# A hybrid transformer layer whose instruction order a planner decides: the planner's constants and ranks, the way six batches are transposed, and the engine that writes a mask

## The chip, the cores and the metric

The kernel runs on one core of one Trainium2 chip, in one launch, all in float32. The metric is the device time of a run in microseconds (us). A separate execution was taken with the hardware profiler; its span runs from the first to the last instruction.

## The reference, cut to what matters

Eight sequences (batches) `x` of 256 tokens by 256 features pass through four residual steps, each on a layer norm of `x`:

```
x = x + attn_a(layernorm(x))   # 16 heads of 128: q, k, v, softmax, output projection
x = x + ffn(layernorm(x))      # gene lookup, see below
x = x + attn_b(layernorm(x))   # 16 heads of 16, rotary, causal mask by blocks of 64 tokens
x = x + ffn(layernorm(x))      # the same weights again
```

For each token, `ffn` computes 512 gene logits from the RMS-normed token, keeps the 32 largest, takes their softmax, sums the chosen gene vectors (32 numbers) with these weights, and multiplies `tanh(. Wd)`, the normed token and `. Wu`. With 256 tokens the block mask of `attn_b` comes down to this: a query of an earlier block of 64 doesn't see a later block.

## The kernel before, in words

**Tiling.** A batch is two tiles (t = 0, 1) of 128 tokens by 256 features. The tiles of a batch are `x[b, t]`. Each step of a batch depends on the step before it, so TensorE is kept busy by running attention A of later batches beside the gene layers (`ffn`, layer 0 and layer 2) and block attention (`attn_b`, layer 1) of earlier ones.

**Who sets the order.** Every operation is first recorded by `do(...)` (L297) with its engine, a cost in ns (how long it occupies the engine, and when its result can be used), the keys it reads and writes, its buffers and a rank. `Plan.order` (L129) then walks through a model of the five queues (PE, DVE, ACT, POOL, SP) and picks, engine by engine, the operation of lowest rank among those that could start within `WAIT` of the earliest. The instructions are emitted in that order and every engine executes its own list strictly in order. So the constants of the model time nothing on the chip, but they decide which instruction stands before which. In the model a consumer on another engine may start `HOP` after its producer's end (and `LOAD` later on PE); a consumer on the same engine (L203) as soon as the engine is free. A DMA lands its transfer time (bytes over `SCATTER` for the trips below) plus `FLIGHT` after it starts to move. `keep_warm` (L213) puts idle transposes of the identity (L1392) where the model leaves PE idle for over 800 ns and a PSUM bank is free.

**Ranks.** PE ranks of attention A are its batch plus the share of heads done (0 to 8). Those of the gene layers and of block attention stand in `PE_RANK`, nearly all negative, so they go first on PE as soon as the model calls them ready. `EW_RANK` does the same for the operations on the other engines and on SP: a small number goes ahead of attention A, one of 20 and more behind it.

**A DRAM trip** (`turn`, L494) transposes without TensorE. VectorE transposes each 128x512 tile in blocks of 32x32 (L510), SP sends four stripes to DRAM (D<-T, L519), and one DMA brings them back permuted (PT<-D, L528). Its flat form (L516, L526) serves a 256-wide normed tile: four stripes of 64 KB out, in pieces of 32 numbers, and four DMAs back. SP waits in order: an instruction that waits for a landing holds all behind it. Trips are used for attention A's probabilities (L708, read by the attend matmuls L721), for its normed input (AxT), for block attention's probabilities (L1265, read by L1292) and, for batches 0 to 4, for the gene weights (L954, read by L992).

**The gene layer** (`ffn` L937, `experts` L1045) has a chain per tile: statistics and norm (L461 to L480, two small steps on POOL); two PE transposes of the normed tile `Fxn` (L1054); a ScalarE copy out of PSUM (L1060); logits (L1068); four rounds of max-8 (L1078) and match-replace (L1095) on VectorE; one pass that keeps the chosen weights (L1100); their transposition; L992, L1012; then the gating (L1025 to L1041).

**Block attention** (`attn_b` L1120): transposes of `Rxn` (L1134), q and k (L1152), rotary on VectorE and POOL, scores of 4 groups (L1228). For each group VectorE then writes the mask's value into 64 rows of the score bank (L1242), takes the row maxima (L1344), and ScalarE the exponentials (L1350). The two tiles of a batch and all batches go through it one after the other (`lane`).

**The last batch** (b = 7) runs attention A tile by tile (L767): all of tile 0, then tile 1, whose last output projection is L876 and whose last addition to `x` is L884. Only the layers of batch 7, and whatever the order has left, come after it.

Of the kernel before, what the change touches and what calls it, by code (L numbers as in the profile page):

```python
# [17 lines left out]
P = 128  # L18
# [15 lines left out]
    [[-0.85, -0.85], [-0.84, -0.84], [-0.83, -0.83]],  # L34
    [[-0.82, -0.82], [7.03, -0.81], [8.72, -0.8]],
    [[7.78, -0.79], [8.7, -0.78], [7.32, -0.77]],
]
EW_RANK = [
    [[1.62, 1.49], [20.64, 2.07], [2.72, 20.2]],
    [[2.79, 3.31], [3.38, 3.19], [21.34, 1.84]],  # L40
    [[22, 4.66], [21.53, 22.1], [3.28, 4.32]],
    [[22.77, 23], [4.69, 23.1], [5.73, 23.2]],
    [[24.18, 5.62], [4.78, 23.98], [6.79, 4.31]],
    [[25.44, 6.57], [5.62, 7.27], [25.2, 7.37]],
    [[8.15, 6.17], [7.09, 26.01], [29.52, 26.55]],
    [[9.27, 8.68], [26.56, 26.64], [7.38, 9.82]],
# [26 lines left out]
class Plan:  # L73
# [4 lines left out]
    HOP = 65.0  # L78
    LOAD = 300.0
    DRAIN = 165.0  # L80
    FLIGHT = 2000.0
    RATE = 330.0
    SCATTER = 200.0
    OPEN = 8
    WAIT = {"PE": 50.0, "DVE": 50.0, "ACT": 100.0, "POOL": 200.0, "SP": 400.0}
# [43 lines left out]
    def order(self):  # L129
        engines = ("PE", "DVE", "ACT", "POOL", "SP")  # L130
        free = dict.fromkeys(engines, 0.0)
        ready = {e: [] for e in engines}
        slots = {}
        for o in self.ops:
            for b in o.bufs:
                slots.setdefault(b.tag, [(0.0, i) for i in range(b.bufs)])
                for i in range(b.bufs):
                    if b.pool is not None and (b.tag, i) not in self.tiles:
                        self.tiles[b.tag, i] = b.pool.tile(b.shape, F32, name=f"{b.tag}_{i}")
            if not o.left:  # L140
                ready[o.eng].append(o)
        done = []

        open_ = [0.0] * self.OPEN

        def start(o):
            t = max(free[o.eng], o.ready)
            if o.eng == "SP":
                t = max(t, open_[0])
            need = {}  # L150
            for b in o.bufs:
                if not b.held:
                    need[b.tag] = need.get(b.tag, 0) + 1
            for tag, n in need.items():
                have = slots[tag]
                if len(have) < n:
                    return None
                t = max(t, sorted(have)[n - 1][0])
            return t

        while len(done) < len(self.ops):
            best = None
            for e in engines:
                cand = [(t, o.pri, o) for o in ready[e] if (t := start(o)) is not None]
                if not cand:
                    continue
                now = min(c[0] for c in cand)
                pick = min((c for c in cand if c[0] <= now + self.WAIT[e]), key=lambda c: (c[1], c[2].n))
                if best is None or pick[0] < best[0]:
                    best = pick  # L170
            if best is None:
                raise RuntimeError("no operation can start: " + str([
                    (o.eng, o.pri, [(b.tag, b.held) for b in o.bufs])
                    for e in engines for o in ready[e]][:12])
                    + str({t: len(v) for t, v in slots.items()}))
            t, _, o = best
            ready[o.eng].remove(o)
            o.at = t
            for b in o.bufs:
                if not b.held:  # L180
                    b.held = True
                    have = slots[b.tag]
                    have.sort()
                    b.i = have.pop(0)[1]
                    b.slot = self.tiles.get((b.tag, b.i))
                    b.begin = t
            free[o.eng] = t + o.occ
            if o.eng == "SP":
                self.moved = max(self.moved, t) + o.lat
                end = self.moved + self.FLIGHT  # L190
                open_.append(end + self.HOP)
                open_.pop(0)
            else:
                end = t + o.lat
            for b in o.bufs:
                b.touch -= 1
                b.end = max(b.end, end)
                if not b.touch:
                    slots[b.tag].append((b.end + self.HOP, b.i))
                    self.taken.setdefault((b.tag, b.i), []).append((b.begin, b.end + self.HOP))  # L200
            for u in o.users:
                u = self.ops[u]
                same = u.eng == o.eng and o.eng != "SP"  # L203
                hop = self.HOP + (self.LOAD if u.eng == "PE" else 0.0)
                u.ready = max(u.ready, t + o.occ if same else end + hop)
                u.left -= 1
                if not u.left:
                    ready[u.eng].append(u)
            done.append(o)
        self.span = max(free.values())  # L210
        return done
# [27 lines left out]
def kernel(  # L239
# [44 lines left out]
    def dve(cols, half=False):  # L284
        occ = 70.0 + cols * (0.52 if half else 1.04)
        return occ, occ + 90.0

    def act(cols, ptr=False):
        occ = 60.0 + cols * 0.833 + (90.0 if ptr else 0.0)
        return occ, occ + 110.0  # L290
# [162 lines left out]
    def normed(b, t, who, ew, rms=False, xn=None, after=(), held=()):  # L453
# [7 lines left out]
            "DVE", (330, 420), lambda: [nc.vector.bn_stats(st(), x())],  # L461
            ew, [(x, 0), *((y, 0) for y in after)], [(st, 0)],
        )
        do("DVE", (90, 175), lambda: [nc.vector.bn_aggr(mv(), st())], ew, [(st, 0)], [(mv, 0)])
# [4 lines left out]
            "POOL", (220, 270),  # L469
# [4 lines left out]
            "POOL", (520, 560),  # L474
# [19 lines left out]
    def turn(sources, dst, n, pri, keys, flat=False):  # L494
# [8 lines left out]
        for j, (p, view) in enumerate(sources):  # L503
            def out(j=j):
# [4 lines left out]
                "DVE", dve(n * P),  # L509
# [23 lines left out]
    def normed_a(b):  # L533
# [35 lines left out]
        if b:  # L569
            for i, (a_, b_, f_) in enumerate((  # L570
# [4 lines left out]
                    "POOL", (480.0, 530.0),  # L575
# [320 lines left out]
    def softmax(sc, keys, p, n, k, who, ew):  # L896
# [9 lines left out]
        for i in range(n):  # L906
            do(
                "ACT", (155 + k * 0.83 + 92, 155 + k * 0.83 + 200),
                lambda i=i: [nc.scalar.activation(  # L909
                    p()[:, i, :], s3()[:, i, :], AF.Exp, bias=nm()[:, i : i + 1],  # L910
                    accum_out=sm()[:, i : i + 1])],
                ew, [*keys, (nm, 0)], [(p, ("e", i)), (sm, i)],
            )
        do(
            "DVE", (75, 165), lambda: [nc.vector.reciprocal(sm(), sm())],  # L915
# [21 lines left out]
    def ffn(b, ts_, layer):  # L937
# [8 lines left out]
        for t, xn, e, sm in zip(ts_, xns, es, sms):  # L946
            experts(
                b, t, layer, lambda stage, t=t: pe(stage, t), xn, e, sm, xns, es, [xs[b, i] for i in ts_])
# [47 lines left out]
        cost = 730.0 if n == 2 else 505.0  # L996
# [12 lines left out]
        cost = 1140.0 if n == 2 else 858.0  # L1009
# [11 lines left out]
    def gated(b, t, ew, pg, down, up, xn, sm):  # L1021
# [7 lines left out]
            "DVE", (390, 490),  # L1029
# [5 lines left out]
            b, t, 256, (700, 740),  # L1035
# [4 lines left out]
            b, t, 256, (690, 730),  # L1040
# [4 lines left out]
    def experts(b, t, layer, pe, xn, e, sm, xns, es, both):  # L1045
# [3 lines left out]
        normed(b, t, "F", ew, True, xn, both, xns)  # L1049
        xT = sb([P, DC, P], "FxT", 2)  # L1050
        pt = bank("B")
        do(
            "PE", (218.0, 218.0 + plan.DRAIN),
            lambda: (nc.tensor.transpose(pt()[:, ts(c, P)], xn()[:, ts(c, P)], ident)  # L1054
                     for c in range(DC)),
            pe(0), [(xn, 0)], [(pt, 0)], [xT, *es],
        )
        do(
            "ACT", act(256),
            lambda: [nc.scalar.copy(xT().rearrange("p c q -> p (c q)"), pt()[:, :S])],  # L1060
            ew, [(pt, 0)], [(xT, 0)],
        )
        pl = bank("B")
        left = sb([P, G], "Fleft", 2)
        for c in range(DC):
# [3 lines left out]
                    pl(), xT()[:, c, :], wcT[:, c, :], start=c == 0, stop=c == DC - 1)],  # L1069
                pe(1), [(xT, 0), ("wcT",)], [(pl, 0)], [left, *es],  # L1070
# [3 lines left out]
        for r in range(4):  # L1074
            src, key = (pl, (pl, 0)) if r == 0 else (left, (left, 0))
            do(
                "DVE", (600 if r else 640, 740 if r else 760),
# [3 lines left out]
            if r == 0:  # L1081
                do(
                    "DVE", (55, 150),
# [5 lines left out]
                    "ACT", (690, 800),  # L1089
# [4 lines left out]
                "DVE", (672, 755),  # L1094
# [4 lines left out]
            "DVE", (720, 820),  # L1099
# [4 lines left out]
        do("DVE", (75, 165), lambda: [nc.vector.reciprocal(sm(), sm())], ew, [], [(sm, 0)])  # L1104
# [6 lines left out]
    kbs = {}  # L1111
    VP = DIM + DB
# [7 lines left out]
    def attn_b(b, t):  # L1120
# [26 lines left out]
        for i, n in enumerate("qk"):  # L1147
# [12 lines left out]
            "DVE", (620, 720),  # L1160
# [11 lines left out]
            b, t, 512, (1235, 1280),  # L1172
# [6 lines left out]
            b, t, 512, (1230, 1275),  # L1179
# [4 lines left out]
        for par in range(2):  # L1184
            vec(
                b, t, 256, (460, 520),
# [26 lines left out]
        def scores(c, pT):  # L1213
# [7 lines left out]
            def emit():  # L1221
# [11 lines left out]
                "PE", (1200.0, 1200.0 + plan.DRAIN), emit, pe(3),  # L1233
# [4 lines left out]
            for g in range(NR):  # L1238
                sc, p = scs[g], ps_[g]
                do(  # L1240
                    "DVE", (n * 53 + 93, n * 53 + 180),
                    lambda sc=sc: [nc.vector.memset(  # L1242
                        sc()[0:BLOCK].rearrange("p (h k) -> p h k", h=n)[:, :, 512 // n - BLOCK :],
                        MASKED)],
# [35 lines left out]
        def attend(cs_, pT):  # L1280
# [17 lines left out]
            cost = 1200.0 if n * len(cs_) == 2 else 650.0  # L1298
# [39 lines left out]
    def softmax_b(sc, p, p3, n, k, ew):  # L1338
# [8 lines left out]
        for i in range(n):  # L1347
            do(
                "ACT", (155 + k * 0.83 + 92, 155 + k * 0.83 + 200),
# [6 lines left out]
            "DVE", (75, 165), lambda: [nc.vector.reciprocal(sm(), sm())],  # L1356
# [92 lines left out]
```

## Time and profile before

| | us |
|---|---|
| three runs, median (lowest, highest) | 959.45 (958.21, 959.88) |
| the profiled execution's own time | 960.78 |
| its span, first to last instruction | 959.0 |
| its time outside the span | 1.78 |
| TensorE clock granted, mean | 0.995 |

| engine | busy us | share of span |
|---|---|---|
| PE (matmul) | 919.5 | 96% |
| VectorE | 703.6 | 73% |
| ScalarE | 468.0 | 49% |
| POOL | 404.4 | 42% |
| DMA queue of SP | | 49.2% of 16 engines |

A matmul in float32 goes through PE in two passes, and each pass is one record; records of neighbours overlap, so PE's busy share is no measure of useful work. The distance from one start to the next is: 216 ns for a pass of 256 columns, 429 for one of 512, 110 for one of 128 or a transpose. Groups of instructions are shown as line, engine, operation, tiles, shape, count | busy us, mean ns of one | idle time of the engine just before them and what ended it.

### The profile page before, as it was taken

How to read it: one execution, taken by the hardware profiler on the slowest of the kernel's cores; microseconds unless marked ns; L12 is line 12 of the kernel's file. 1: busy time of each engine (PE TensorE's matmuls, PEld its weight loads, DVE VectorE, ACT ScalarE, POOL GpSimd, SP SyncE). 2: the span in 40 equal slices, each digit the busy share in tenths (PEclk: the TensorE clock that was granted, in tenths of full speed). 3: DMA queues.
4: the chain of work that ended last, by engine and by line, in shares of the span. 5: the costliest groups of instructions: out<-in, count | busy, mean ns of one | idle time of the engine just before them, and what ended most of it. 6: DMA issues, size and time to landing. Idle time of an engine off the chain costs nothing.

```text
span 959.0 us, 17226 instructions
## 1 busy us (share of the span) xinstructions
PE 919.5 (96%) x5815; PEld 737.7 (77%) x5815; DVE 703.6 (73%) x1716; ACT 468.0 (49%) x1550; POOL 404.4 (42%) x530
## 2 busy tenths in 40 slices
PE   7999999999999999999999999999999999999776
PEld 6878888887678777887678788877777877787564
DVE  2543484769967789669886884988788788868765
ACT  3534343754266544564455554465436643764461
POOL 4722224642176422662247343464237414743430
PEclk9999999999999999999999999999999999999989
DMA  9873333476337763485455746177525731550000
GB/s 324 248 209 94 110 106 115 123 221 173 111 111 200 202 166 105 131 231 174 135 143 171 200 133 190 44 208 216 148 67 163 211 106 40 147 173 1 6 7 12
DMA packets 109192, 136.09 MB, mean 142 GB/s; under 512 B 26288, under 2 KB 90416, under 8 KB 109104
## 3 DMA queue, kind: packets, MB, share of 16 engines
q1 hardware_dynamic: 109104, 134.99, 49.2%
q8 instruction: 46, 0.75, 0.3%
q14 instruction: 42, 0.34, 0.1%
HBM read 72.82 MB, written 62.13 MB: 141 GB/s over the span
## 4 chain that ended last, share of the span: by engine, by line
PE 56%; DVE 32%; issue 4%; DMA 3%; POOL 2%; ACT 2%; SPq 1%; DVEq 0%; ACTq 0%
PE ps L674 12%; DVE Fleft L1095 8%; DVE Fm L1078 7%; PE ps L696 7%; PE ps L721 6%; PE ps L595 5%; PE ps L743 5%; DVE T L510 4%; PE ps L1068 2%; PE ps L1228 2%; DMA D<-T 2%; PE ps L1152 2%; DVE Bnm L1344 2%; DVE Fe L1100 2%; PE ps L789 2%
## 5 line engine op out<-in xcount | busy, mean ns | idle before, releaser
L920 POOL TENSOR_TENSOR p<-p,Asm 128x512 f32<-128x512 f32 x128 | 135.1, 1058 | 266.0 <-DVE Asm L915 262.7
L674 PE MATMUL ps<-AxT,wqk 128*128 128x256 f32 x896 | 222.6, 382 | 0.2 <-ACT Fe L1090 0.2
L674 PEld LDWEIGHTS ps<-AxT,wqk 128*128 128x128 f32 x896 | 169.9, 191 | 26.6 <-issue 3.5
L909 ACT ACTIVATE p<-ps,Anm 128x256 f32<-128x256 f32 x256 | 119.5, 474 | 106.7 <-DVE Anm L903 97.1
L510 DVE STREAM_TRANSPOSE T<-p 128x512 f32<-128x512 f32 x202 | 133.4, 689 | 11.6 <-POOL p L920 7.6
L1361 POOL TENSOR_TENSOR p<-p,Bsm 128x512 f32<-128x512 f32 x96 | 99.1, 1047 | 84.6 <-DVE Bsm L1356 84.1
L903 DVE TENSOR_REDUCE Anm<-ps 128x2 f32<-128x512 f32 x128 | 86.4, 678 | 52.0 <-PE ps L696 49.3
L696 PE MATMUL ps<-Aqk 128*128 128x256 f32 x448 | 119.6, 382 | 1.4 <-ACT Aqk L683 0.9
L1350 ACT ACTIVATE p<-ps,Bnm 128x128 f32<-128x128 f32 (+1 forms) x256 | 105.4, 445 | 30.9 <-DVE Bnm L1344 23.5
L743 PE MATMUL ps<-woutT,Aao 128*128 128x256 f32 x448 | 111.0, 383 | 1.4 <-ACT Aao L731 1.0
L721 PE MATMUL ps<-PT,Av 128*128 128x256 f32 x448 | 108.5, 382 | 0.2 <-DMA PT<-D 0.2
L683 ACT ACTIVATE Aqk<-ps 128x512 f32<-128x512 f32 x112 | 66.9, 605 | 69.1 <-PE ps L674 68.5
L743 PEld LDWEIGHTS ps<-woutT,Aao 128*128 128x128 f32 x448 | 82.9, 190 | 21.7 <-issue 6.6
L721 PEld LDWEIGHTS ps<-PT,Av 128*128 128x128 f32 x448 | 83.7, 190 | 17.3 <-issue 4.3
L696 PEld LDWEIGHTS ps<-Aqk 128*128 128x128 f32 x448 | 83.1, 190 | 17.3 <-ACT Aqk L683 3.6
L595 PE MATMUL ps<-wv,Ax 128*128 128x256 f32 x224 | 66.7, 386 | 2.6 <-ACT Av L616 1.8
L1344 DVE TENSOR_REDUCE Bnm<-ps 128x2 f32<-128x512 f32 (+1 forms) x96 | 66.2, 690 | 2.7
L1078 DVE MAX8 Fm<-Fleft 128x8 f32<-128x512 f32 x96 | 66.4, 692 | 2.4
L1095 DVE MATCH_REPLACE8 Fleft<-Fm,Fleft 128x512 f32<-128x512 f32 x96 | 64.8, 675 | 0.0
L616 ACT COPY Av<-ps 128x256 f32<-128x256 f32 x108 | 40.6, 376 | 46.8 <-PE ps L595 46.5
L1068 PE MATMUL ps<-wcT,FxT 128*128 128x512 f32 x128 | 60.8, 601 | 0.0
L1350 ACT ACTIVATION_READ_ACCUMULATOR p<-ps,Bnm 128x1 f32 x256 | 58.6, 229 | 0.0
(130 smaller groups left out, 1405.6 us busy)
## 6 DMA issues: line engine op xcount, KB each, us to landing
D<-T SPq DMA_DIRECT2D x444, 128.0 KB, 2.6
PT<-D SPq DMA_DIRECT2D x111, 512.0 KB, 4.1
wqk<-in_wqkvT_dram SPq DMA_DIRECT2D x8, 512.0 KB, 9.7
x<-in_x_dram SPq DMA_DIRECT2D x16, 128.0 KB, 3.4
wv<-in_wqkvT_dram SPq DMA_DIRECT2D x4, 512.0 KB, 10.0
woutT<-in_woutT_dram SPq DMA_DIRECT2D x4, 512.0 KB, 10.6
out_dram<-x SPq DMA_DIRECT2D x16, 128.0 KB, 2.0
D<-T SPq DMA_DIRECT2D x28, 64.0 KB, 3.1
```

The costliest lines, as they stand in the source:

```text
L510: lambda out=out, view=view: [nc.vector.transpose(*view(out()))],
L595: lambda: [nc.tensor.matmul(dst(), a(), w_, start=start, stop=True, skip_group_check=not start)],
L674: lambda kind=kind, c=c: [nc.tensor.matmul(pq()[:, ts(kind, S)].rearrange("p (t q) -> p t q", t=TT), wA[kind, g][:, c, ts(i, DA)], xT.row( ...
L696: lambda t=t: [nc.tensor.matmul(sc()[:, ts(t, S)], qk()[:, 0, ts(t, P)], qk()[:, 1, :], start=True, stop=True)],
L721: lambda j=j, k=k, g=g, i=i: [nc.tensor.matmul(po()[:, ts(j, S)].rearrange("p (t g q) -> p t g q", t=TT, g=4), vs[g]()[:, AT[k, i // 2], t ...
L743: lambda t=t, h=h: [nc.tensor.matmul(py()[:, ts(t, DIM)], ao[h - h % 2]()[:, h % 2, ts(t, P)], woutT[:, h, :], start=h == hs[0], stop=h == ...
L909: lambda i=i: [nc.scalar.activation(p()[:, i, :], s3()[:, i, :], AF.Exp, bias=nm()[:, i : i + 1], accum_out=sm()[:, i : i + 1])],
L920: lambda: [nc.gpsimd.tensor_tensor(p(), p(), sm().unsqueeze(2).to_broadcast((P, n, k)), ALU.mult)],
L1078: lambda r=r, src=src: [nc.vector.max(m8[r](), src())],
L1095: lambda r=r, src=src: [nc.vector.match_replace(left(), m8[r](), src(), TAKEN)],
L1350: lambda i=i: [nc.scalar.activation(p3()[:, i, :], s3()[:, i, :], AF.Exp, bias=nm()[:, i : i + 1], accum_out=sm()[:, i : i + 1])],
L1361: lambda: [nc.gpsimd.tensor_tensor(p3(), p3(), sm().unsqueeze(2).to_broadcast((P, n, k)), ALU.mult)],
```

## The change

1. The model of the planner. `HOP` is split by the consumer's engine (35 to 79 ns, 65 before) and a buffer is free 40 ns after its last use. A consumer on the same engine now waits for its producer's end, except on PE. `FLIGHT` goes from 2000 to 1600, `SCATTER` from 200 to 290, SP's `WAIT` from 400 to 200, and many single costs are set anew (most by under 10%).
2. New `PE_RANK` and `EW_RANK`.
3. In `ffn`, both tiles of a batch are normed first and share one `FxT` tile. For batches 0 to 5 (`by_trip`) a flat trip takes the place of the PE transposes (L1054) and copies (L1060). The other batches keep them.
4. The mask: ScalarE copies a constant tile `hidden` into the score bank where VectorE wrote it by memset (L1242).

The sums and the data that each step computes are as before.

```diff
-    HOP = 65.0
+    HOP = {"PE": 60.0, "DVE": 35.0, "ACT": 60.0, "POOL": 79.0, "SP": 60.0}
+    FREE = 40.0
-    FLIGHT = 2000.0
+    FLIGHT = 1600.0
-    SCATTER = 200.0
+    SCATTER = 290.0
...
-                same = u.eng == o.eng and o.eng != "SP"
-                hop = self.HOP + (self.LOAD if u.eng == "PE" else 0.0)
+                same = u.eng == o.eng == "PE"
+                hop = self.HOP[u.eng] + (self.LOAD if u.eng == "PE" else 0.0)
                 u.ready = max(u.ready, t + o.occ if same else end + hop)
...
+        by_trip = n == 2 and b < B - 2
+        xT = sb([P, TT, S], "FxT", 1)
+        for t, xn in zip(ts_, xns):
+            normed(b, t, "F", first(b, t, layer), True, xn, [xs[b, i] for i in ts_], xns)
+        if by_trip:
+            turn(
+                [(xn, lambda T, xn=xn: (
+                    T.rearrange("p c (k q) -> p k c q", k=DC),
+                    xn().rearrange("p (k c q) -> p k c q", k=DC, c=4))) for xn in xns],
+                lambda: xT().rearrange("p t s -> p (t s)"), DC, first(b, ts_[-1], layer),
+                [(xT, i) for i in range(n)], flat=True,
+            )
...
+    hidden = ctile([BLOCK, 4, BLOCK], "hidden")
+    nc.gpsimd.memset(hidden, MASKED)
...
-                    "DVE", (n * 53 + 93, n * 53 + 180),
-                    lambda sc=sc: [nc.vector.memset(
+                    "ACT", act(n * BLOCK),
+                    lambda sc=sc: [nc.scalar.copy(
                         sc()[0:BLOCK].rearrange("p (h k) -> p h k", h=n)[:, :, 512 // n - BLOCK :],
-                        MASKED)],
+                        hidden[:, :n, :])],
```

## The prediction

> **What bounds the kernel now.** I read the page first, then busy time by stretch, then matmuls by start times, then the chain of waits from its end.
>
> ```profile
> span 959.0 us, 17226 instructions
> PE 919.5 (96%) x5815; PEld 737.7 (77%) x5815; DVE 703.6 (73%) x1716; ACT 468.0 (49%) x1550; POOL 404.4 (42%) x530
> ...
> PEclk9999999999999999999999999999999999999989
> ```
>
> ```profile
> 0.00:40.00 40.00, 34.80 (x137) 27.35 (x138) 13.54 (x35) 16.55 (x48) 24.94 (x43) 1.00 0.94 309
> 40.00:870.00 830.00, 816.83 (x5100) 659.95 (x5099) 627.33 (x1523) 414.64 (x1387) 351.80 (x452) 1.00 0.53 148
> 870.00:883.40 13.40, 12.15 (x61) 8.25 (x61) 11.21 (x30) 6.13 (x17) 4.29 (x6) 1.00 0.01 2
> 883.40:959.00 75.60, 55.72 (x523) 42.16 (x520) 51.50 (x130) 30.69 (x102) 23.35 (x30) 0.94 0.02 8
> ```
>
> The columns are the stretch, its length, busy us (instructions) of PE, weight loads, VectorE, ScalarE and POOL, clock, DMA share, GB/s. Up to 870 PE sets the pace; in the last stretch PE is padded with idle transposes and the chain runs through VectorE. The border is PE's last attention projection:
>
> ```profile
> 880.80 1.46 PE L876 MATMUL ps<-woutT,Aao 128*128 128x256 f32 x6
> 882.87 0.44 PE L1134 MATMUL ps<-ident,Rxn 128*128 128x128 f32 x2 [0.60 <-DVE Rxn L480]
> ```
>
> It ends at 882.3. I call that the **border** and the 76.7 us behind it the **tail**. Pricing matmuls by their start distances (216, 429, 110 ns; 35 and 28 for the packed ones of L1228 and of L1292 and L992), real PE work up to the border is 827.8 us in the program's order. The other 54.5 are 8.4 idle and 0.9 padding at the head, and some 45 us of holes: 16.5 in holes over 300 ns (4.8 of them before L966, 3.2 before L595, 2.3 before L1134, 1.0 before L1054), the rest of 15 to 300 ns, at hand-overs.
>
> **What moves.** The order of the changed program, priced by the same distances, has 816.3 us of real PE work ahead of the border: 11.5 less. The transposes L1054 fall from 64 to 16 matmuls: 48 x 110 ns = 5.3 us gone for good. The other 6.2 are batch 6's second gene layer, which now stands behind the border. If holes per matmul stayed, the border would be at 882.3 - 11.5 = 870.8.
>
> ```profile
> L1054 PE MATMUL ps<-ident,Fxn 128*128 128x128 f32 x64 | 12.7, 284 | 3.4 <-DVE Fxn L480 3.2
> L1060 ACT COPY FxT<-ps 128x256 f32<-128x256 f32 x32 | 12.1, 381 | 13.6 <-PE ps L1054 13.3
> L1242 DVE MEMSET ps<- 64x128 f32 x64 | 10.6, 165 | 11.8 <-PE ps L1228 10.8
> L1242 DVE MEMSET ps<- 64x256 f32 x32 | 8.7, 272 | 6.4 <-PE ps L1228 5.1
> L510 DVE STREAM_TRANSPOSE T<-Axn 128x256 f32<-128x256 f32 x14 | 5.4, 419 | 2.0 <-DMA D<-T 2.0
> ```
>
> Other engines: VectorE loses 96 memsets (10.6 + 8.7 = 19.3 us) and gains 24 block transposes (24 x 0.419 = 10.1). ScalarE loses 24 copies (9.1) and gains 96 mask copies. No row shows a copy from SBUF into PSUM; the nearest are copies out of PSUM, 0.266 for 128 columns (L1308) and 0.381 for 256, so 64 x 0.27 + 32 x 0.38 = 29.5 us; the memsets' times are the low end (19.3), twice the copy the high end (59). ScalarE goes to 468 + 20 = 488, still half idle; the copy sits where the memset sat, and the next group's copy runs beside this group's reduction (0.69), so ahead of the border I price it at nothing. Without that cover it would be 0.3 per group, 2.4 us for the eight in the last tile.
>
> **Term 1, holes that close: -4.** A VectorE result was planned as ready for VectorE when the engine was free, some 0.08 to 0.1 us too early per step, and max-8 and match-replace make eight such steps. So L966, L1054 and L1134 stood too early on PE: 8 us of the large holes. The new model waits for the end. Bounds 0 (other latenesses are behind it) and -8; I take half, since L966 of the last batches keeps its form and other late inputs.
>
> **Term 2, holes that open: +8.** This is the change's danger. The new constants plan a 128 KB x 4 trip at 6.9 us from VectorE's last transpose to the landing (four stripes of 0.45, flight 1.6, return 1.8, flight 1.6), where the old ones planned 9.2 (4 x 0.66 + 2.0 + 2.6 + 2.0).
>
> ```profile
> D<-T SPq DMA_DIRECT2D x444, 128.0 KB, 2.6
> PT<-D SPq DMA_DIRECT2D x111, 512.0 KB, 4.1
> ...
> D<-T SPq DMA_DIRECT2D x28, 64.0 KB, 3.1
> AxT<-D SPq DMA_DIRECT2D x28, 64.0 KB, 2.2
> ```
>
> Followed one by one (53 trips whose stripes go alone), the trace has median 7.5, quarters 6.9 and 8.5. The old plan was 1.7 us late at the median, the new one is 0.6 early, and PE runs in order: an attend placed too early stops it. Today the data are there a median 3.3 us before L721 asks, 5.8 before L1292, 2.4 before L992. Taking 2.4 us off each wait, what falls below zero sums to 12.5 us on 46 of the 56 attends followed, so 15 on all, 4 before L1292, 5 before L992: 24. The order agrees: between a head's scores and its attend lie a median 13.1 us of PE work (lowest 11.4), against 20.9 (14.0); the quickest such chain in the trace took 11.0, a crowded one 15.6. The 12 new flat trips are planned at 5.9; the seven of AxT took 7.8 at the least, and the logits L1068 come first on PE as soon as planned: up to 12 x 1.9 = 23 more, if nothing covers them; with L992's other slack (2.4 - 1.7 = 0.7) and PE's own lateness against the plan (the 29 us of small holes, 0.45 per 13 us) about 0.25 each, 3. So 27 in all if the shortfalls added up. They don't: a hole for one trip gives its length to every other trip in flight. Some 100 returns in 830 us are one per 8.3, and a chain lasts 13 and more, so two or three share one hole: 27 / 3 = 9, less what PE's lateness covers, 8. Bounds 0 and 27.
>
> SP is a queue of its own: 96 more issues (48 out, 48 back) of 0.44 us are 42 us, on about 260 now, plus a wait for each landing with everything behind it held. That is in the share above.
>
> For the 64 KB pieces of 32 numbers (128 bytes) the row says 3.1 us against 2.6 for twice the bytes. The Trainium skill, "DMA: Bandwidth & Descriptors", Specifications, asks for at least 512 bytes per piece for full rate and says that smaller ones cost a read-modify-write, which speaks against these trips; the row agrees. Its section "Anatomy of one DMA — SWDGE (gpsimd) path" gives 2.0 us plus bytes / 436 GB/s, an estimate of 2.15 for 64 KB; by it a flat trip would be 1 us shorter and the sum 2 to 3 us lower. The measured 3.1 decides.
>
> **Term 3, the tail: 78.0 instead of 76.7.** VectorE has 63.3 us of work behind the border by its rows (52.2 before by the same rows, 51.5 measured): batch 6's two gene tiles add 13.5, twelve memsets of the mask go (2.4). I walked its order from the border, each operation at its row (max-8 0.71, match-replace 0.77, reductions 0.69, each with its hand-over):
> - tile 1's addition, norm, two POOL steps (0.76), transposes, copy and logits: first max-8 at 6.0; its four rounds, with 2 us of others between, and the last pass: 14.2; transposes, copies, L992 and L1012 (3.5, as in the end below), gating: 19.9;
> - reductions, rotary, batch 6's two gene tiles, interleaved, VectorE never idle: 49.1;
> - block attention's return (POOL scaling, transposes, copies, projection, addition) and logits: 55;
> - two gene tiles of layer 2, interleaved: 70.
>
> ```profile
> 950.06 0.71 DVE Fe L1100 x2
> ...
> 950.82 0.66 PE ps L966 x4
> ...
> 954.30 0.50 DVE Fup L1030
> ...
> 955.78 0.43 DVE x L1041
> ```
>
> From the last pass's end (950.77) to the span's end are 8.2 us now, so 78. The batch 6 tiles fill time in which VectorE waits today (76.7 - 51.5 = 25).
>
> **Sum.** 882.3 - 11.5 - 4 + 8 + 78.0 = 952.8 span; with 1.78 outside it 954.6, against the profiled execution's 960.78, which lies 1.33 above the median of the runs. At the median: **953**.
>
> **Rivals**, all at the median (span + 0.45).
> - *The order simply fits better*: no new holes, 8 us of old ones gone. 882.3 - 11.5 - 8 + 78.0 = 940.8, so 941. For it: the fewer large memset and DVE steps, and 5.8 us to spare at L1292. Against: the 7.5 us trips.
> - *The planned slack was what kept PE fed* (the other side): trips land after PE asks for them, at L721, L992 and the logits, all over 40 to 870. Price 27 with nothing closing: 882.3 - 11.5 + 27 + 78.0 = 975.8, so 976. It turns the sign once new holes less closed ones pass 12.1 us (870.8 + 12.1 + 78.0 + 0.45 = 961.4). For it: 0.6 us early at the median, 11.4 against chains of 11.0 to 15.6. Against: holes are shared.
> - *The tail isn't filled*: VectorE's 25 us of waiting stay and the added work comes on top: 63.3 + 25.2 = 88.5; 870.8 + 4 + 88.5 = 963.3, so 964. Against: the walk, where independent gene tiles stand between dependent steps.
> - *The change doesn't do what it says*: excluded, the counts in the order are as told.
>
> **Chances.** A measurement of this kernel tells 0.2% (1.9 us) from no change, so faster is below 957.5, slower above 961.4. Forecast (946 to 957.5) 0.40; better fit 0.22; between the lines 0.12; tail 0.08; holes 0.18. Faster 0.62, same 0.12, slower 0.26. The range reaches from the better fit's 940 into the holes' case, to 969, about 0.1 left out on each side; the forecast's own is 946 to 957.5.
>
> **What would show it.** Border at about 875 and tail near 78: right. L721, the logits and L992 with idle time put down to PT<-D and FxT<-D beyond 10 us: the holes. VectorE under 70% busy behind the border: the tail. L966, L1054 and L1134 with as much idle time ahead of them as now: term 1 wrong. ScalarE's mask copy far from 0.27 and 0.38, or reductions waiting for it, would make the copies' zero wrong.

## The result: slower, and where the time came from

The changed kernel took 986.19 us (median of four runs, 980.33 to 988.58) against 958.83 for the kernel before on the same chip (958.15 to 959.88). The ratio, estimated from all these runs, is 1.0275, 95% interval [1.0228, 1.0323]. The profiled execution took 988.58, the slowest of the four; its span is 986.7.

In the new numbering, L721 (attend), L1292 (block attend), L1068 (logits), L992 (gene sums) are L722, L1308, L1082, L1020; L966, L1054 and L1134 are L994, L965 and L1150; L876 is L877; the mask is L1258, the row maxima L1360.

First the page, then busy time by stretch (length, then PE, weight loads, VectorE, ScalarE, POOL with their instructions, clock, DMA share, GB/s), then the last attention projection in the timeline:

```profile
span 986.7 us, 17393 instructions
PE 925.1 (94%) x5783; PEld 736.2 (75%) x5783; DVE 674.2 (68%) x1644; ACT 482.4 (49%) x1622; POOL 407.0 (41%) x531
...
PEclk9999999999999999999999999999999999999999
```

```profile
40.00:900.00 860.00, 818.36 (x4982) 654.62 (x4981) 595.18 (x1440) 425.13 (x1443) 352.69 (x449) 0.99 0.54 148
...
912.00:986.70 74.70, 61.90 (x569) 45.45 (x569) 57.20 (x149) 36.13 (x121) 27.91 (x38) 0.99 0.03 8
```

```profile
911.29 0.70 PE L877 MATMUL ps<-woutT,Aao 128*128 128x256 f32 x2
```

PE has less to do and stands still more: 95.2% busy between 40 and 900 us, where it was 98.4% between 40 and 870. The border moved from 882.3 to 912.0, the tail shrank from 76.7 to 74.7. So the whole loss lies ahead of the border. Matmuls by their start distances split it, with the same prices as in the prediction (holes counted from 40 us on, those under 15 ns left out; work counted from the records of the traces, padding all the way to the border, so the row of before differs a little from the prediction's 827.8 and 0.9):

| ahead of the border, us | before | after |
|---|---|---|
| real PE work | 828.5 | 817.0 |
| padding; idle at the head | 1.5; 8.4 | 1.8; 6.9 |
| holes of 15 to 300 ns | 26.4 | 32.3 |
| holes over 300 ns | 16.5 | 53.2 |
| of these: PE fed by a DMA trip (attend, block attend, logits, gene sums) | 0.3 | 48.9 in 43 holes |
| of these: all others | 16.2 | 4.3 |

Who PE waited for, from the view of waits (us in total, times, longest). Before:

```profile
PE ps L966 <- DVE Fe L1100: 7.1, 8, 2.2
...
PE ps L1134 <- DVE Rxn L480: 4.5, 5, 2.1
```

After:

```profile
PE ps L722 <- DMA PT<-D: 19.0, 19, 3.4
PE ps L1308 <- DMA PT<-D: 9.0, 7, 2.7
...
PE ps L1082 <- DMA FxT<-D: 5.2, 3, 2.9
PE ps L1020 <- DMA PT<-D: 4.2, 4, 2.7
...
PE ps L994 <- DVE Fe L1114: 2.2, 2, 1.1
```

The waits for VectorE's results went down, as meant. In their place stand waits for landings, which the kernel before had nearly none of. (This view counts idle time between records, which overlap, and the tail too; the table goes by start distances. So the sums differ.) Following 46 attends in one trace and 50 in the other, the data lay ready a median 3.4 us before the attend started; now it is 0.13, that is, most attends start as the data land. One of them in the timeline, SP's issues (SPq) and the attend:

```profile
286.28 5.65 SPq L529 DMA_DIRECT2D PT<-D  x2
...
290.24 0.73 PEld L722 LDWEIGHTS ps<-PT,Av 128*128 128x128 f32 x4 [3.84 <-DMA PT<-D]
290.24 1.13 PE L722 MATMUL ps<-PT,Av 128*128 128x256 f32 x4 [3.44 <-DMA PT<-D]
```

PE stood 3.44 us for one return. The trips themselves hardly got slower (issue to landing, us):

```profile
D<-T SPq DMA_DIRECT2D x444, 128.0 KB, 2.8
PT<-D SPq DMA_DIRECT2D x111, 512.0 KB, 4.0
D<-T SPq DMA_DIRECT2D x76, 64.0 KB, 2.3
```

They were 2.6, 4.1 and 3.1. From VectorE's last transpose to the landing a lone four-stripe trip took a median 7.6 us against 7.5. Nor does the data come later after the scores: from the end of a pair's scores to the landing of its return it took a median 14.2 us, and 16.4 before (42 and 33 of the 56 attends, those whose return the semaphores in the trace identify). It is PE that asks earlier.

VectorE asks earlier too. Its transposes write the tile `T`, which is free again when the stripes of an earlier trip have landed. Before, and after:

```profile
L510 DVE STREAM_TRANSPOSE T<-p 128x512 f32<-128x512 f32 x202 | 133.4, 689 | 11.6 <-POOL p L920 7.6 <-DMA D<-T 2.2 <-POOL p L1361 0.5
```

```profile
L511 DVE STREAM_TRANSPOSE T<-p 128x512 f32<-128x512 f32 x202 | 134.9, 693 | 27.7 <-DMA D<-T 20.2 <-POOL p L921 4.6 <-POOL p L1377 1.5
```

With the other tiles that it transposes, VectorE stood 29.3 us for landings, 4.2 before. The same wait is 25.9 us in e2 below, where only the two DMA constants are changed, and 5.9 in e1, where only they are set back. The prediction didn't look at it.

The chain of work that ended last shows the same: it ran 3% of the span through DMA before, and now

```profile
PE 53%; DMA 18%; DVE 12%; SPq 6%; POOL 3%; issue 3%; ACT 3%; DVEq 0%; ACTq 0%; POOLq 0%
```

### The profile page after: what moved, and what is told of

Read it like the earlier page. It is cut to its first block, busy times and chain, and to the rows that moved or that the text cites. A ratio compares the mean times of both kernels' runs of the same rounds, so it can differ in the third digit from the quotient of the medians.

```text
span 986.7 us, 17393 instructions
## 1 busy us (share of the span) xinstructions
PE 925.1 (94%) x5783; PEld 736.2 (75%) x5783; DVE 674.2 (68%) x1644; ACT 482.4 (49%) x1622; POOL 407.0 (41%) x531
## 2 busy tenths in 40 slices
DMA packets 136841, 142.39 MB, mean 144 GB/s; under 512 B 52400, under 2 KB 116528, under 8 KB 136752
## 4 chain that ended last, share of the span: by engine, by line
PE 53%; DMA 18%; DVE 12%; SPq 6%; POOL 3%; issue 3%; ACT 3%; DVEq 0%; ACTq 0%; POOLq 0%
DMA PT<-D 10%; PE ps L675 10%; DMA D<-T 7%; PE ps L744 6%; PE ps L722 6%; PE ps L697 5%; PE ps L596 4%; SPq L520 4%; PE ps L1082 3%; DVE T L511 3%; PE ps L1168 2%; DVE Fleft L1109 2%; PE ps L1244 2%; PE ps L860 2%; PE ps L1040 1%
## 5 line engine op out<-in xcount | busy, mean ns | idle before, releaser
L675 PEld LDWEIGHTS ps<-AxT,wqk 128*128 128x128 f32 x896 | 169.3, 190 | 23.5 <-issue 1.0
L722 PE MATMUL ps<-PT,Av 128*128 128x256 f32 x448 | 110.9, 388 | 20.2 <-DMA PT<-D 19.0
L722 PEld LDWEIGHTS ps<-PT,Av 128*128 128x128 f32 x448 | 83.0, 191 | 45.7 <-DMA PT<-D 17.4
L1360 DVE TENSOR_REDUCE Bnm<-ps 128x2 f32<-128x512 f32 (+1 forms) x96 | 61.5, 678 | 30.8 <-ACT ps L1258 30.8
L1082 PE MATMUL ps<-wcT,FxT 128*128 128x512 f32 x128 | 61.5, 617 | 6.3 <-DMA FxT<-D 5.2
L1092 DVE MAX8 Fm<-Fleft 128x8 f32<-128x512 f32 x96 | 64.2, 681 | 0.5
L732 ACT COPY Aao<-ps 128x512 f32<-128x512 f32 x56 | 33.0, 589 | 59.2 <-PE ps L722 59.0
```

Source lines behind the costliest of these rows:

```text
L675: lambda kind=kind, c=c: [nc.tensor.matmul(pq()[:, ts(kind, S)].rearrange("p (t q) -> p t q", t=TT), wA[kind, g][:, c, ts(i, DA)], xT.row( ...
L722: lambda j=j, k=k, g=g, i=i: [nc.tensor.matmul(po()[:, ts(j, S)].rearrange("p (t g q) -> p t g q", t=TT, g=4), vs[g]()[:, AT[k, i // 2], t ...
L1082: lambda c=c: [nc.tensor.matmul(pl(), part(c), wcT[:, c, :], start=c == 0, stop=c == DC - 1)],
```

## The experiments

**Theory A**: the two DMA constants, FLIGHT and SCATTER, move PE's DMA-fed matmuls forward in the order, so that they ask before the data land; the rest of the change is harmless or good. **Rivals**: B, the flat trips crowd SP and the DMA queue; C, the new ranks; D, the mask on ScalarE; E, SP and the DMA queue can't carry more, so that PE waits for a rate and not for a landing asked for too early. FLIGHT and SCATTER were always moved together: what each does alone stays open. Every edit makes the planner lay out the whole order anew, and the tail swings with it (75 to 125 us), since the ranks were fitted to another plan. So I read the border and its holes beside the time.

All times are medians, each with its ratio to the kernel before, run beside it on the same chip. "Room" is the median PE work that the order puts between a head pair's scores and its attend; "ready" how long before the attend the data lay there (median, in the trace). Holes, border and tail are those of the profiled execution, which lies up to 5 us off the median of its kernel.

| run | us | ratio [95%] | room | ready | DMA-fed holes | other holes over 0.3 | border | tail |
|---|---|---|---|---|---|---|---|---|
| before (profiled run) | 958.8 | 1 | 20.9 | 3.4 | 0.3 | 16.2 | 882.3 | 76.7 |
| after | 986.2 | 1.0275 [1.0228, 1.0323] | 13.1 | 0.13 | 48.9 | 4.3 | 912.0 | 74.7 |
| e1 after, old constants | 996.7 | 1.0394 [1.0372, 1.0415] | 18.6 | 3.2 | 0 | 4.9 | 866.8 | 124.6 |
| e2 before, new constants | 1003.4 | 1.0459 [1.0421, 1.0498] | 13.5 | 0.4 | 35.4 | 12.3 | 926.9 | 79.7 |
| e3 after, no flat trips | 994.7 | 1.0367 [1.0333, 1.0401] | 13.8 | 0.5 | 30.6 | 10.3 | 912.8 | 84.9 |
| e4 after, old ranks | 1003.0 | 1.0451 [1.0429, 1.0473] | 13.1 | 0.35 | 40.7 | 10.9 | 920.1 | 82.5 |
| e7 after, mask by memset | 1001.4 | 1.0433 [1.0402, 1.0465] | 13.7 | 0.2 | 45.4 | 5.3 | 905.5 | 96.0 |
| e10 after, halfway constants | 959.2 | 0.9996 [0.9984, 1.0008] | 15.6 | 1.4 | 9.9 | 8.7 | 872.5 | 84.5 |
| e11 after, old constants, ranks fitted | 932.0 | 0.9704 [0.9690, 0.9719] | 22.3 | 3.2 | 0 | 2.7 | 848.7 | 80.6 |
| e12 before, hold alone | 939.9 | 0.9795 [0.9780, 0.9810] | 18.9 | 3.7 | 0 | 0 | 855.1 | 82.9 |
| e13 as e11, no hold | 987.3 | 1.0293 [1.0277, 1.0308] | 21.2 | 3.3 | 1.7 | 23.3 | 883.9 | 101.3 |
| e14 halfway, ranks fitted | 948.7 | 0.9880 [0.9855, 0.9904] | 15.4 | 1.5 | 14.7 | 4.6 | 869.3 | 78.8 |

**The constants, taken out (e1) and put in alone (e2).**

```diff
 e1, in the changed kernel            e2, in the kernel before
-    FLIGHT = 1600.0                 -    FLIGHT = 2000.0
+    FLIGHT = 2000.0                 +    FLIGHT = 1600.0
-    SCATTER = 290.0                 -    SCATTER = 200.0
+    SCATTER = 200.0                 +    SCATTER = 290.0
```

> The changed kernel with two constants of the plan set back: FLIGHT 2000, SCATTER 200. The order then has a median 18.6 us of PE work between scores and attend (13.1 in the changed kernel, 20.9 before), and 807.9 us of PE work ahead of the border. Theory A (the planned speed of the DMA trips opens the holes): holes over 300 ns ahead of the border fall from 53 to under 20 us, the time to 940 to 960. Rival B (the 12 flat trips load SP and stop the logits): above 975, since all trips stay. Rival C (the new ranks fit badly): above 975, since the ranks stay.

> The kernel before with only FLIGHT 1600 and SCATTER 290 in its plan. Scores to attend falls from a median 20.9 to 13.5 us of PE work. Theory A: the holes before L721, L1292 and L992 appear without any other part of the change, 25 to 45 us of them, and the time is 980 to 1000. Rival B: there are no flat trips for the gene layers here, so no change beyond 5 us: 955 to 965. Rival C: ranks are those of before: 955 to 965.

e1: every DMA-fed hole over 0.3 us is gone and the border is at 866.8. The time is no better all the same, above 975 as rivals B and C had said and far from theory A's 940 to 960: the plan left work to the tail, 124.6 us long, and padded PE with 24.6 us ahead of the border. With the same constants and ranks fitted to them (e11) that is gone. e2 is the cleaner half: two numbers changed in the kernel before bring 44 us (1003.4, 3 us above the range given) and the new kind of wait.

```profile
PE ps L721 <- DMA PT<-D: 15.1, 16, 2.0
...
PE ps L1292 <- DMA PT<-D: 5.9, 7, 1.4
```

The kernel before has no flat trip in the gene layers, none of the new ranks, no mask copy; the constants are enough to make it.

**The rivals, each undone in the changed kernel (e3, e4, e7).**

```diff
 e3, the PE transposes again
-        by_trip = n == 2 and b < B - 2
+        by_trip = False
 e4: PE_RANK and EW_RANK of the kernel before
 e7, the memset again
-                    "ACT", act(n * BLOCK),
-                    lambda sc=sc: [nc.scalar.copy(
+                    "DVE", (n * 53 + 93, n * 53 + 180),
+                    lambda sc=sc: [nc.vector.memset(
```

> The changed kernel without the flat trips of the gene layers (all batches by PE transposes and copies, one shared FxT tile). Scores to attend stays at 13.8 us. Theory A: the 8.6 us of holes before the logits go, 5.3 us of PE work come back, the holes of the other trips stay: 975 to 988. Rival B: the holes go with the trips, 950 to 965. Rival C: above 975.

> The changed kernel with both rank tables of before. Scores to attend stays at 13.1 us. Theory A: the holes stay, 970 to 995. Rival B: 970 to 995 as well. Rival C: the ranks were the cause, so 945 to 962.

> The changed kernel with the mask written by VectorE's memset again, planned with its old cost. Theory A: the mask is a side matter, 978 to 994 (every edit re-plans the order). Rival D (the row maxima now wait for ScalarE's copies, 31 us of VectorE's idle time in the changed kernel, and the block attention's chain is longer for it): 955 to 972.

None of the three lowers the time; all three lie 7 to 8 us above theory A's range, so the whole time wasn't forecast well, with every edit laying out the order anew. In each the DMA-fed holes stay at 30.6 to 45.4 us, with 13.1 to 13.8 us of room. Without the flat trips, the logits' 8.6 us of holes are gone, but the border doesn't move (912.8): the trips are not the cause, though they share in its price. e3's time alone would fit rival C as well; e2, with the ranks of before, and e4 speak against C.

**Moving the DMA-fed matmuls back by hand (e5, e6, e8, e9).** The finished order of the changed kernel was sorted anew, with each matmul that a trip feeds 2 us (e5, e8) or 4 us (e6, e9) later and whatever depends on it or on its buffers behind it; in e8 and e9 what follows also keeps its planned distance.

```diff
+                if o.eng == "PE" and o.n in fed:
+                    k += by
+                for p in before.get(o.n, ()):
+                    k = max(k, key[id(p)])                            # e5, e6
+                    k = max(k, key[id(p)] + min(o.at - p.at, p.lat))  # e8, e9
...
+        return sorted(done, key=lambda o: key[id(o)])
```

> The changed kernel with its own plan, in which afterwards only the PE operations fed by a DRAM trip (and what depends on them) are set 2 us later in the order; all constants, ranks, trips and the mask stay. Scores to attend goes from a median 13.1 to 14.3 us of PE work, VectorE's order stays nearly the same. Theory A (PE asks for the trips too early): the holes before L722, L1308, L1020 and L1082 fall from 49 us to 15 to 30, the border from 912 to about 885 to 895, the time to 960 to 975. Rival E (the trips are late because SP and the DMA queue can't carry more, so PE waits for a rate and not for a latency): what PE no longer waits for at one trip it waits for at the next, the time stays within 980 to 990.

> The same with 4 us. Scores to attend 15.6 us. Theory A: the holes fall further, under 15 us, 950 to 970. Rival E: 980 to 990.

> The edit before last, mended: PE operations fed by a DRAM trip are set 2 us later in the changed kernel's own order, and what depends on them keeps its distance from them (in the first form the copies behind them were set at the matmuls' own time, so ScalarE stood before matmuls that had not run, and the scores and projections waited for ScalarE instead: L697's and L744's lines opened 103 us of holes, while those at the four DMA-fed lines fell to nothing). Theory A: the DMA-fed holes fall from 49 to 15 to 30 us with no new ones, the time to 955 to 975. Rival E (a rate and not a latency): 980 to 995.

> The same with 4 us. Theory A: DMA-fed holes under 15 us, 945 to 970, if the tail stays near 75. Rival E: 980 to 995.

All four are far slower, outside every range given: 1100.9, 1250.1, 1063.4 and 1135.7 us (ratios 1.1482 [1.1463, 1.1501], 1.3041 [1.3015, 1.3068], 1.1070 [1.1049, 1.1091], 1.1826 [1.1808, 1.1843]). The DMA-fed holes went, to 2.5, 1.1, 5.1 and 0.6 us. But other holes took their place, 39.6 us of them before the scores in e8 and 32.6 before the projections. A stretch of e8's timeline (in this kernel L702 is q and k, L711 the copy, L724 the scores):

```profile
406.32 0.59 PE L623 MATMUL ps<-wv,AxT 128*128 128x256 f32 x2
406.58 0.60 ACT L711 ACTIVATE Aqk<-ps 128x512 f32<-128x512 f32 x1 [2.07 <-PE ps L702]
...
407.23 0.30 PEld L724 LDWEIGHTS ps<-Aqk 128*128 128x128 f32 x2 [0.72 <-ACT Aqk L711]
```

ScalarE had been free for 2.07 us and copied at once; PE had only one pair of matmuls to fill the copy's 0.60 us and two hand-overs with. The 39 such holes are 1.0 us each. It seems that the attends had filled these gaps in the planner's order. So this test tells nothing for or against theory A or rival E as to the total: an order can't be loosened at one kind of matmul alone.

**Degree, and ranks that fit (e10, e11, e14).** e10 and e14 have the constants halfway, e11 the old ones; e11 and e14 also have both rank tables fitted anew, each to its own plan.

```diff
 e10, e14 (e11: 2000.0 and 200.0)
-    FLIGHT = 1600.0
+    FLIGHT = 1800.0
-    SCATTER = 290.0
+    SCATTER = 245.0
 e11, batch 0 of PE_RANK
-    [[-1, -1], [-0.99, -0.99], [-0.98, -0.98]],
+    [[-1.0, -1.0], [0.58, -0.99], [-0.03, 0.38]],
...
```

> The changed kernel with the planner's two DMA constants halfway back (FLIGHT 1800, SCATTER 245), nothing else changed. The order then puts 15.6 us of TensorE work (median) between a turn's scores and its attend, against 13.1 in the changed kernel, 18.6 with the old constants and 20.9 in the kernel before; ahead of the border TensorE has the changed kernel's work (816.5 against 816.3 us). Theory A (the room that the two constants leave for the trip is what was lost): the DMA-fed holes of over 0.3 us (attend, block attend, logits, gene sums) come to between 5 and 25 us in place of 48.9, each wait being shorter by up to 2.5 us, and the border stands at 870 to 890. If only the constants' full old value keeps TensorE fed, the holes stay at 40 to 50 and the border at 905 to 915. The tail is not forecast: the ranks were not fitted to this plan.

> The changed kernel with the old DMA constants (FLIGHT 2000, SCATTER 200) and ranks PE_RANK and EW_RANK fitted anew to that plan; results held until their producer ends, flat trips and mask copies stay as in the changed kernel. Its order has 22.3 us of TensorE work (median) between scores and attend (kernel before 20.9), 814.1 us of work ahead of the border and 38.5 behind. Theory A: DMA-fed holes of over 0.3 us under 6 us, all holes ahead of the border 35 to 45, so the border at 855 to 868; with a tail of 75 to 85 (the ranks fitted, unlike those of the run with the constants alone) a span of 930 to 953: faster than both kernels. Rival: the run with the old constants alone had no DMA-fed holes only because its order was loose everywhere; with work packed tightly again they return, border 890 or later, span 965 or more.

> The changed kernel with the DMA constants halfway (FLIGHT 1800, SCATTER 245) and ranks fitted anew to that plan. 15.4 us of TensorE work (median) between scores and attend, 816.5 ahead of the border. Theory A: DMA-fed holes of over 0.3 us as in the halfway run, 5 to 15 us, all holes 35 to 46, so a border at 853 to 866 and, with a tail of 75 to 82, a span of 930 to 946: faster than both kernels, but 3 to 15 us slower than the version with the old constants and fitted ranks. Rival: with ranks that fit, halfway is as good as the old constants or better, a span of 930 or less.

e10: with 2.5 us more of room than the changed kernel, the DMA-fed holes are 9.9 us in place of 48.9, the border is at 872.5, both within theory A's ranges, and the time is that of the kernel before. From its waits:

```profile
PE ps L722 <- DMA PT<-D: 3.2, 3, 1.8
PE ps L1082 <- DMA FxT<-D: 2.9, 3, 1.3
```

e11 beats both kernels: 932.0, 28 us under the kernel before run beside it (960.25), with all of the change in place but the two constants and the ranks. Its chain by engine and its attend group:

```profile
PE 81%; DVE 13%; POOL 3%; ACT 2%; issue 1%; DMA 0%; DVEq 0%; POOLq 0%; ACTq 0%
...
L722 PE MATMUL ps<-PT,Av 128*128 128x256 f32 x448 | 108.2, 380 | 0.0
```

The rival (a tightly packed order brings the holes back) falls: the border of 848.7 is the lowest of all, with no DMA-fed hole. Rivals B and E fall with it: all flat trips are there and the same traffic (136,842 packets, 136,841 in the changed kernel) goes through in 929.3 us of span, without PE waiting for it. Border and span came out 6 and 1 us better than the ranges given. e14 lies 16 to 17 us above e11; of the 20.6 us by which its border stands later, 14.7 are DMA-fed holes. It is slower than I had expected, the border by 3 us and the span by 2, and 16 to 17 us behind e11 in place of 3 to 15. The rival, that halfway is as good once the ranks fit, isn't borne out; how well either fit came out is not on record.

**The hold (e12, e13).**

```diff
 e12, in the kernel before
-                same = u.eng == o.eng and o.eng != "SP"
+                same = u.eng == o.eng == "PE"
 e13: the reverse, in e11's kernel
```

> The kernel before with one part of the change alone: a consumer on the same engine waits in the model for its producer's end (except on PE). Constants, ranks, transposes and mask as before. The order keeps 18.9 us of TensorE work (median) between scores and attend (before 20.9); 821.8 us of work stand ahead of the border in place of 827.8. Theory A with term 1 right: the holes of over 0.3 us ahead of L966, L1054 and L1134, 8.1 us in the kernel before, fall to under 4; no DMA-fed holes to speak of (under 3), so a border at 868 to 874. If these three wait for other late inputs, they stay at 6 to 9 and the border is at 875 to 879. The tail is not forecast, since 6 us more of TensorE work stand in it.

> The fitted version (old DMA constants, new ranks) with the hold undone: a consumer on the same engine is again planned as soon as the engine is free. The ranks were fitted to the plan with the hold, so the tail is not forecast; the order has 808.1 us of work ahead of the border in place of 814.1, and 44.5 behind in place of 38.5. Theory A: DMA-fed holes stay under 4 us (21.2 us of work between scores and attend). Term 1: holes of over 0.3 us where TensorE waits for VectorE's results (L965, L994, L1150, 1.8 us with the hold) come back to 5 to 10 us. If the hold does nothing, they stay under 3.

One line takes the kernel before from 959.64 to 939.94. I had expected a border at 868 to 874; it is at 855.1, because not only the holes ahead of L966, L1054 and L1134 are gone, but all 16.5 us of holes over 0.3 us, and 5.6 us of the small ones, beside the 6 us of work that I had expected to move behind the border. The chain:

```profile
PE 91%; DVE 6%; ACT 1%; issue 1%; POOL 1%; DMA 0%; DVEq 0%; ACTq 0%
```

The holes before L595, L696 and L743 (6.3 us before) waited mostly for ScalarE's copies; the hold also plans ScalarE's own successors, which would explain them, but that was not tried apart, and the new order itself may have closed some. e13 is the counterpart: L994, L965 and L1150 come back to 8.1 us (5 to 10 expected), all holes over 0.3 us from 2.7 to 25.0. Who waits there (the whole span):

```profile
PE ps L994 <- DVE Fe L1114: 13.3, 8, 3.4
```

Its 987.3 us also hold a tail of 101.3 and 16.1 us of padding, as in e1 from ranks fitted to another plan; so the hold's worth is read from e12 and the holes, not from e13's time.

What separates e11 from e12 (7 to 9 us by the ratios) is flat trips, mask, ranks and the model's other new constants together; that was not taken apart.

## Why the prediction was wrong, step by step

**The border's work: right.** Predicted 11.5 us less ahead of the border; measured 828.5 - 817.0 = 11.5.

**Term 1, holes that close: right in kind, too small.** Predicted -4, bounds 0 and -8. Holes other than the DMA-fed ones fell by 16.2 - 4.3 = 11.9 us in the changed kernel and by 16.2 with the hold alone, with 5.6 of small ones besides. The step looked at three lines where TensorE waits for VectorE; with the hold alone all others closed as well (e12). In the changed kernel the small holes went the other way, 26.4 to 32.3.

**Term 2, holes that open: this step failed.** Predicted +8, bounds 0 and 27; measured +48.6 over 0.3 us. Piece by piece, before sharing, against the holes measured: attends 15 and 23.5, block attends 4 and 12.0, gene sums 5 and 4.8, logits 3 and 8.6. The mechanism was right, an attend placed too early stops PE; its size was not. The step that failed is "Taking 2.4 us off each wait". 2.4 us is by how much the constants shorten one planned trip. By how much they move PE's matmuls stood in the next sentence of the same paragraph, 20.9 to 13.1 us of work, taken there as agreement; it is 7.8. The traces show the same shift: from the scores' end to the attend's start, the median of the elapsed time fell from 21.8 to 14.7 us, with the last part of that waited out. By the prediction's own list of waits, 7.8 us off each of the 46 attends followed would have been 182 us before sharing, 2.4 off was 12.5. (The planned trip of 6.9 adds up to 6.8 by the prediction's own terms; against 9.2 that is the 2.4.)

The prediction set that planned time against the median of lone trips, 7.5, and called it 0.6 early. Of all 111 four-stripe trips in the trace of before, paired in order with VectorE's transposes, the fastest took 6.9 us and the median 10.2, since most share SP with another; after, 7.0 and 9.3. So the new plan gave a trip no more than the fastest one needed. The same stands in the rows of single transfers: a stripe is planned at 0.45 + 1.6 = 2.05 us and took 2.6, a return at 1.8 + 1.6 = 3.4 and took 4.1. The flat trips were planned at 5.9; the twelve of the changed kernel took 7.5 at the least, 9.8 at the median.

The other half of the step, "27 / 3", erred the other way, if anything: the attends' holes came to 23.5 us, so if every attend had moved by 7.8 us, about eight waits shared a hole (182 / 23.5), not three. That is a reckoning; the sharing was not followed hole by hole. The two errors offset in part, and the bound of 27, got from the small shift, was no bound. What goes with the holes in these runs is how long the data lie ready: 3.2 us or more at the median go with 0 to 1.7 us of holes, 1.4 and 1.5 with 9.9 and 14.7, 0.13 to 0.5 with 30.6 to 48.9.

Why 2.4 us per trip become 7.8 is shown for the constants as a whole (e2: 20.9 to 13.5, with nothing else changed), and only argued for the way: the smallest distance fell by 2.6 (14.0 to 11.4), about the trip's own part, and the bulk moved down onto it. In the model a transfer starts when the last one has moved, so SCATTER also sets how long trips queue for each other. By the model's prices, the 444 stripes and 111 returns of the four-stripe trips take 582 us of its one queue at SCATTER 200 and 401 at 290. That this planned queueing was the room that PE lost is my reading; no run moves SCATTER alone.

**The rival that happened.** "The planned slack was what kept PE fed" names this mechanism and three of its four places rightly (block attention, 12.0 us of holes, it doesn't name), at 0.18 and a price of 27. As bookkeeping, with the measured price (48.6, and 5.9 of small holes, less 11.9 closed) its own sum gives a border of 870.8 + 42.6 = 913.4; 912.0 was measured.

**Term 3, the tail: right in kind.** Predicted 78.0, measured 74.7. VectorE is busy 57.2 us of it (77%), predicted 63.3: the trace has 20 max-8 behind the border (15 before), where batch 6's two gene tiles would have made 23. With the border 30 us late, part of batch 6 was done by then. So 6.1 us less work stood against 2.8 us more waiting (17.5 against 14.7), and the near hit is in part luck. From the last pass's end (978.1) to the span's end it takes 8.6 us (8.2 before), along the same steps.

**The mask at nothing: nothing speaks against it, but it isn't isolated.** Copies by form, and the reductions' waits for them:

```profile
L1360 DVE TENSOR_REDUCE Bnm<-ps 128x2 f32<-128x512 f32 x64 | 41.3, 677 | 9.6 <-ACT ps L1258 9.6
...
L1360 DVE TENSOR_REDUCE Bnm<-ps 128x4 f32<-128x512 f32 x32 | 20.2, 680 | 21.2 <-ACT ps L1258 21.2
...
L1258 ACT COPY ps<-hidden 64x128 f32<-64x128 f32 x64 | 13.9, 263 | 10.7 <-PE ps L1244 10.6
...
L1258 ACT COPY ps<-hidden 64x256 f32<-64x256 f32 x32 | 10.5, 366 | 8.7 <-PE ps L1244 8.7
```

24.4 us of copies against 29.5 estimated (its products add up to 29.4). The reductions do wait for them, 30.8 us in all, which the prediction named as a sign against its zero; but VectorE doesn't set the pace ahead of the border, and with the memset back (e7) the border came 6.5 us earlier (2.3 of it work that moved behind it, 3.5 fewer DMA-fed holes in a new order), and the tail grew by 21.3. What is left, 0.7 us, is too little to tell from the effect of a new order, so a price of the copies ahead of the border isn't seen; in the tail the new order hides it.

## What to carry to other kernels

When an order is made by a planner, a constant's effect is read from the order that comes out (how much work lies between producer and consumer), not from the constant's size, and set against how long the data lie ready in the trace; a few us of that slack, where a DMA feeds an in-order engine, are worth more than a tighter plan. A median landing time of lone trips is no safe thing to plan with: the halfway constants plan such a trip at 7.9 us (4 x 0.535 + 1.8 + 2.14 + 1.8), above the median of 7.5, and still leave 9.9 and 14.7 us of DMA-fed holes (e10, e14); the old constants' 9.2 leaves next to none (0 to 1.7 us in the kernel before, e1 and e11 to e13). After a change of the planner's constants the ranks have to be fitted again before a total says anything about the part that was changed; until then the holes are what to read.

## What the runs showed of the hardware

- A ScalarE copy from SBUF into PSUM on 64 partitions takes 0.263 us for 128 columns and 0.366 for 256, about as long as one out of PSUM (0.266 and 0.381 before, on 128 partitions).
- 64 KB stripes in pieces of 128 bytes landed after 2.3 us (median of 76) where the trace of before had 3.1 (28), and 128 KB stripes took 2.8. So the penalty for small pieces that the prediction read out of its row, as in the Trainium skill, "DMA: Bandwidth & Descriptors", Specifications, isn't seen in the changed kernel; nor in e12, where the same 28 stripes as before took 2.2. That page's section "Anatomy of one DMA — SWDGE (gpsimd) path" gives 2.15 us as an estimate for 64 KB, and the changed kernel's 2.3 lies near it; but the trace lists these transfers, which SP issues, under the queue hardware_dynamic, so that is no test of the page's figure.
- The flat trips doubled the packets under 512 bytes (26,288 to 52,400) and raised all packets from 109,192 to 136,841, and the median lone four-stripe trip still took 7.6 us against 7.5.
